# Four graph layers in one kernel: order edges in layer 0, matmuls on zeros ahead of it, and a weight fold spread between transposes

## The chip, the cores and the metric

The kernel runs on one NeuronCore of one Trainium2 chip. The metric is the device time of one execution in microseconds, as a median over runs. "PE" is the matrix engine (TensorE), "DVE" the vector engine, "ACT" the scalar engine, "POOL" GpSimd, and "SP" the engine whose queue issues most of the transfers. "PEclk" is the share of the full clock that the chip granted the PE.

## What is computed

The inputs are x (128 graphs, 64 nodes, 256 features) and adj (128, 64, 64). Four residual layers follow each other, each ending in a layernorm over the features:

- Layer 0: five groups of nodes (one of 25 nodes, the others of 9, 7, 6 and 6), all among the first 25. Each group has its own two-layer graph convolution on the group's part of adj, with weights W1 (256 to 512) and W2 (512 to 256). The outputs are weighted by softmax(fusion_w) and added into the group's nodes.
- Layer 1: one graph convolution with the whole normalised adjacency.
- Layer 2: a polynomial of degree three in the row-normalised adjacency, with a leaky ReLU.
- Layer 3: five rounds of messages, each a GRU cell: gates from `m @ w_ih.T` and `h @ w_hh.T`, where m is the sum over neighbours of `h @ weight[l]`.

The core of layer 0:

```
def _graph_conv(x, adj, W, b):
    A = adj + jnp.eye(n)
    deg = jnp.sum(A, axis=-1)
    dinv = jnp.where(deg == 0, 0.0, deg_safe ** (-0.5))
    norm_adj = dinv[:, :, None] * A * dinv[:, None, :]
    support = jnp.einsum('bnd,de->bne', x, W)
    out = jnp.einsum('bnm,bme->bne', norm_adj, support) + b
    return jax.nn.relu(out)
```

All arithmetic is in f32.

## The kernel before

**Layer 0 in units.** The graphs of a group are cut into units of up to four tiles (class Unit): several graphs' nodes stand below each other on up to 126 partitions. There are 16 units, in the order of the groups 1, 2, 3, 4, 0: three, two, two, two and seven of them. For each unit these steps run:

- `load0`: the group's rows of adj into tile a (three buffers) and of x into xg (six buffers). The loads go out from SP's queue, for units 0 to 2 xg from POOL's; unit 0 uses ACT's queue for half of its a loads.
- `prep`: on DVE, ae = a + identity (L374), its row sums deg, their inverse root (L118 to L124, with a power on POOL, L122), ae scaled (L382), and A0, the block-diagonal matrix of the tile's graphs, made by a multiplication with the constant block0 (L385). The PE transposes A0 (pT, L393), and DVE scales and evicts it to AT (L397). The list `evictions` holds these instructions, `powers` the powers.
- `aggregate`: pa = x times the adjacency (PE, L407), copied by ACT to ag (L412).
- `hidden`: ph = W1 times ag (PE, L422), ReLU by ACT to hg (L425).
- `support`: ps = hg times W2 (PE, L436), copied by ACT to s (L442).
- `add`: po = s times the adjacency (PE, L458), ReLU by ACT to z (L462), added on DVE to F (L469, L480).
- `finish`, for group 0 only: z transposed back (pse, L493), added to x, layernorm, and stored to xa.

The loop is a software pipeline: in iteration i the PE gets add(i-1), aggregate(i+1), support(i), finish(i-1), prep(i+2), hidden(i+1), in this order. Between these it places, from unit 9 on, the steps of layers 1 and 2 for the first two chunks (`early`, that is mid(0) and mid(1); a chunk is eight graphs). Beside the loop stand the layernorms of the nodes 25 to 63 (`others`, tiles xo, one in most iterations), which go out to xb. mid(c) begins with the whole adjacency of its chunk (a64, loaded at L190): Ab (L225), its mask A01 (L231), rsum (L233), then dg (L243) and, on ACT, poly (L247).

**After layer 0.** `fold()` forms V[l], the product of weight[l] and w_ih, in 15 steps (products pf, PE L546; copies by ACT to w, L685, and following). `factors` then forms, for each, sums that the GRU's matrix products use: three on DVE (L662, L664, L665) and one on POOL (L663). The same is done for w_hh. Then come the first states' transposes (`state_of_layer2`, pT L757) and the first messages (pa, L209), chunk by chunk, and the GRU loop, whose first matmul is called parz (L716).

**What sets the order.** The order on the PE is the program's, written by hand. On the other engines a scheduler orders by dependencies and priority; `tc.issue_after(x)` adds an edge that makes an instruction stand after x, and `tc.high_priority()` moves one forward. Each engine then works through its own order and waits at each instruction until that one's inputs have come. PSUM banks come from two pools in rotation (`psum0`).

Of the kernel before, what the change touches and what calls it, by code (L numbers as in the profile page):

```python
# [9 lines left out]
F32 = mybir.dt.float32  # L10
# [51 lines left out]
NU = len(UNITS)  # L62
XP = 40
EPS_LN = 1e-5


@with_exitstack
def gnn_stack(
# [41 lines left out]

        return const(bass.AP(tensor=src.tensor, offset=src.offset, ap=[[0, 128], [1, n]]), [128, n], name, eng, pool)

    powers, evictions = [], []

    def inv_sqrt(v, n, p, name):

# [215 lines left out]
    with ExitStack() as c0:  # L332
# [9 lines left out]
        def load0(i, after=None):  # L342

            u = UNITS[i]

            qa = [nc.scalar, nc.sync] if i == 0 else [nc.sync]
            qx = nc.gpsimd if i < 3 else nc.sync
            a = work.tile([TR, 4, NJ], F32, name="a", bufs=3)
            xg = work.tile([TR, 4, D], F32, name="xg", bufs=6)
            for t, (b0, nb) in enumerate(u.tiles):  # L350
                b = slice(b0, b0 + nb)
                row = 0
                for f, m in RUNS[u.g]:
                    rows = slice(row, row + nb * m)
                    row += nb * m
                    w = u.n if u.g < 2 else NE
                    qa[t % len(qa)].dma_start(a[rows, t, :w], adj[b, f : f + m, 0:w])
                    with tc.issue_after(after.ins) if after else nullcontext():
                        qx.dma_start(xg[rows, t, :], x[b, f : f + m, :])
            loads[i] = a, xg  # L360

        def prep(i):

            u = UNITS[i]
            a, xg = loads.pop(i)
            ae = work.tile([TR, 4, NJ], F32, name="ae", bufs=2)
            A0 = work.tile([TR, 4, TR], F32, name="A0", bufs=1)
            AT = work.tile([TR, 4, TR], F32, name="AT", bufs=4)
            p = psum0("pT").rearrange("p (t n) -> p t n", t=4)
            scale = []  # L370
            for ts, nb, r, k in u.same:
                w, c = ts.stop - ts.start, 0
                for f, m in [(0, u.n)] if u.g < 2 else RUNS[u.g]:
                    nc.vector.tensor_add(  # L374
                        ae[:r, ts, c : c + m], a[:r, ts, f : f + m], eye0[:r, k, None, c : c + m].to_broadcast([r, w, m])
                    )
                    c += m
                av = ae[:r, ts, : u.n]
                deg = small.tile([TR, w], F32, name="deg")
                nc.vector.tensor_reduce(deg[:r], av, AX.X, ALU.add)  # L380
                dinv = inv_sqrt(deg[:r], w, r, "d0")
                nc.vector.tensor_mul(av, av, dinv[:, :, None].to_broadcast([r, w, u.n]))  # L382
                o, c = 0, 0
                for _, m in RUNS[u.g]:
                    nc.vector.tensor_mul(  # L385
                        A0[:r, ts, o : o + nb * m].rearrange("p t (b n) -> p t b n", n=m),
                        ae[:r, ts, None, c : c + m].to_broadcast([r, w, nb, m]),
                        block0[:r, None, k, o : o + nb * m].rearrange("p t (b n) -> p t b n", n=m)
                        .to_broadcast([r, w, nb, m]),
                    )  # L390
                    o, c = o + nb * m, c + m
                for t in range(ts.start, ts.stop):
                    nc.tensor.transpose(p[:r, t, :r], A0[:r, t, :r], ident[:r, :r])  # L393
                scale.append((AT[:r, ts, :r], p[:r, ts, :r], dinv[:, :, None].to_broadcast([r, w, r])))
            for v in scale:
                with tc.high_priority():
                    evictions.append(nc.vector.tensor_mul(*v))  # L397
            A[i] = AT, xg
# [16 lines left out]
        def hidden(i):  # L415
            u = UNITS[i]
            ag0 = AG.pop(i)
            hg = keep.tile([128, 4, 512], F32, tag="NI", name="hg", bufs=2)
            for e in range(4):
                p = psum0("ph")[:, : u.cols]  # L420
                for k in range(2):
                    nc.tensor.matmul(  # L422
                        p, W1[:, u.g, k, e * 128 : (e + 1) * 128], ag0[:, k, : u.cols], start=k == 0, stop=k == 1
                    )
                nc.scalar.activation(hg[:, e, : u.cols], p, AF.Relu, bias=b1[:, u.g * 4 + e : u.g * 4 + e + 1])  # L425
            HG[i] = hg

        def support(i):
# [84 lines left out]

        def others(i):

            layernorm(XO[i], n=XO[i].shape[1])

        def store_others(i):
            t = XO.pop(i)
            nc.sync.dma_start(xb[:, NP * i : NP * i + t.shape[1], :], t)  # L520

        eye0 = const(c_eye0, [TR, 5, NJ], "eye0", nc.scalar, w0)
        load0(0)
        ident = const(c_ident, [128, 128], "ident", nc.scalar)
        block0 = w0.tile([TR, 5, TR], F32, name="block0")
        for ks in (slice(1, 2), slice(2, 5), slice(0, 1)):
            nc.scalar.dma_start(block0[:, ks], c_block0[:, ks])
        nc.vector.memset(F, 0.0)
        b1 = const(b1T, [128, NG * 4], "b1", nc.scalar, w0)
# [35 lines left out]
        for i in range(-2, NU + 1):  # L565
# [21 lines left out]
            if i == -2:  # L587
                load0(1, powers[0])
                load_second(1)
                load0(2, powers[0])  # L590
                load_first(2)
            elif i == -1:
                load_second(2)
                load_first(3)
            elif i == 0:
                load_second(3)
                for g in (4, 0):
                    load_first(g)
                    load_second(g)
            early_stage(i, 2)  # L600
            for f, j in ((store_others, i - 1), (others, i), (load_others, i + 2)):
                for o in range(10):
                    if min(o + 1, 9) == j:
                        f(o)
            if i == -1:

                with tc.issue_after(evictions[0].ins):
                    fm = small.tile([128, 1], F32, name="fm")
                    nc.vector.tensor_reduce(fm, fw, AX.X, ALU.max, negate=True)
                    fe = small.tile([128, NG], F32, name="fe")  # L610
                    nc.scalar.activation(fe, fw, AF.Exp, bias=fm)
                    fs = small.tile([128, 1], F32, name="fs")
                    nc.vector.reduce_sum(fs, fe, axis=AX.X)
                    fr = small.tile([128, 1], F32, name="fr")
                    nc.vector.reciprocal(fr, fs)
                    gw = w0.tile([128, NG], F32, name="gw")
                    nc.vector.tensor_scalar(gw, fe, fr, None, op0=ALU.mult)
                    gb2 = w0.tile([128, NG, 2], F32, name="gb2")
                    nc.vector.tensor_mul(gb2, b2c.rearrange("p (g k) -> p g k", k=2), gw[:, :, None].to_broadcast([128, NG, 2]))
            elif i == 1:  # L620
# [8 lines left out]
                    bhh = const_later(bhhT, [128, 6], "bhh")  # L629
                    mask = const_later(maskT, [128, B // 2], "mask")  # L630
                brz = wp.tile([128, 4], F32, name="brz")
                nc.vector.tensor_add(brz, bih[:, 0:4], bhh[:, 0:4])
            elif i == 4:

                ih = keep.tile([128, 4, 2, D], F32, tag="RZ", name="ih", bufs=2)
                wl = keep.tile([128, 4, 2, D], F32, tag="RZ", name="wl", bufs=2)
# [20 lines left out]
    WHH = work.tile([128, 3, 7, 128], F32, name="WHH")  # L657
    V = [work.tile([128, 3, 7, 128], F32, name=f"V{l}") for l in range(L)]

    def factors(w, w21):  # L660

        nc.vector.tensor_add(w[:, 4, :], w21, w[:, 3, :])  # L662
        nc.gpsimd.tensor_sub(w[:, 6, :], w[:, 0, :], w21)  # L663
        nc.vector.tensor_sub(w[:, 5, :], w[:, 4, :], w[:, 0, :])  # L664
        nc.vector.tensor_sub(w[:, 2, :], w[:, 1, :], w[:, 5, :])  # L665

    raw21 = []

    def fold():
        w21 = work.tile([128, 3, 128], F32, name="wh21")  # L670
        raw21.append(w21[:, 2, :])
        wv = whhT.rearrange("(k p) (q e) -> k p q e", p=128, q=3)
        nc.gpsimd.dma_start(w21, wv[0, :, :, 128:])
        for k in range(2):
            nc.gpsimd.dma_start(WHH[:, :, k, :], wv[k, :, :, :128])
        nc.gpsimd.dma_start(WHH[:, :, 3, :], wv[1, :, :, 128:])
        for l in range(L):
            for q in range(3):
# [2 lines left out]
                nc.scalar.copy(w[:, 0:2, :], p[:, :, 0:128])  # L681
                nc.scalar.copy(w[:, 3, :], p[:, 1, 128:256])
                kept = l == L - 1 and q == 2
                v21 = work.tile([128, 128], F32, name="kept21") if kept else work.tile([128, 128], F32, name="w21", bufs=2)
                nc.scalar.copy(v21, p[:, 0, 128:256])  # L685
                if kept:
                    raw21.append(v21)
# [59 lines left out]
    class Chunk:  # L747
# [12 lines left out]
        def state_of_layer2(self, k):  # L760
            if k:
                self.hT = work.tile([128, 2, NP * 128], F32, tag="hT", name="hT", bufs=4)
            p = self.transpose(lambda q, k: self.xt[:, q, k * 128 : (k + 1) * 128], k, "pT3")
            nc.scalar.copy(self.hT[:, k, :], p)
            if not k:
                self.th = sums(self.hT, "h")

# [122 lines left out]
    rows = []  # L890
    weights = fold()
    for c in (0, 1):
        for _ in range(6):
            next(weights)
        rows.append(Chunk(c))
        rows[c].state_of_layer2(1)
        rows[c].state_of_layer2(0)
        rows[c].messages()
    for _ in weights:
        pass  # L900
# [128 lines left out]
```

## Time and profile before

The median is 2215.38 us (three runs, 2215.13 to 2219.1); the profiled execution spans 2216.7 us.

| stretch, us | what runs | PE busy | DVE busy | ACT busy | PEclk | DMA share |
|---|---|---|---|---|---|---|
| 0 to 60 | layer 0, units 0 to 2 | 46.19 | 25.03 | 17.01 | 1.00 | 0.61 |
| 60 to 140 | layer 0, groups 2 to 4 | 73.23 | 42.87 | 24.03 | 0.94 | 0.58 |
| 140 to 320 | group 0, first steps of layers 1 and 2 | 180.00 | 87.26 | 66.55 | 1.00 | 0.13 |
| 320 to 352 | fold, first states | 29.69 | 25.42 | 13.18 | 0.95 | 0.15 |
| 352 to 2190 | GRU loop | 1838.00 | 1174.63 | 874.19 | 1.00 | 0.03 |
| 2190 to 2217 | end of the last chunk | 14.35 | 18.97 | 8.88 | 0.83 | 0.12 |

How to read it: busy time is the time in which an engine has an instruction running. In the rows of a timeline the first two numbers are the start and the length; then come the engine, the line of the kernel, the operation, the tiles (written from read), their sizes, the number of instructions gathered into the row and, in brackets, the idle time before it and what ended it. In a row of waits the three numbers are the total, the count and the longest.

### The profile page before, as it was taken

The numbers are of one execution on the slowest core, as the hardware profiler recorded it, in microseconds if no ns is written. First come the engines' busy times: TensorE is split into PE (matmuls) and PEld (weight loads), VectorE is DVE, ScalarE is ACT, GpSimd is POOL, SyncE is SP. The second block draws the span as 40 slices with busy tenths as digits, with TensorE's granted clock in tenths as the row PEclk, the third lists the DMA queues.
The fourth block names the chain that finished last, engine by engine and source line by source line (L and its number), as shares of the span: only waits on it lengthen the run. The fifth ranks groups of instructions, "written<-read, shape, count | busy, mean of one in ns | idle before, by whom it ended". The sixth has DMA issues, their size and how long they took to land.

```text
span 2216.7 us, 30151 instructions
## 1 busy us (share of the span) xinstructions
PE 2181.5 (98%) x11530; PEld 1913.5 (86%) x11530; DVE 1374.2 (62%) x3069; ACT 1003.8 (45%) x1853; POOL 578.5 (26%) x639
## 2 busy tenths in 40 slices
PE   7999999999999999999999999999999999999997
PEld 5677888888898889888889898888898898888886
DVE  4443567666666666666766676657666666566546
ACT  2333334445544444445454454455454544455453
POOL 3210123222222223223222222222222232232221
PEclk9999999999999999999999999999999999999999
DMA  6540210000100000000100010001000000000000
GB/s 188 168 129 19 61 46 3 1 3 1 38 4 3 1 20 22 4 1 1 41 1 3 1 41 1 4 1 41 1 1 1 20 10 1 1 10 10 1 1 20
DMA packets 54172, 51.12 MB, mean 23 GB/s; under 512 B 20878, under 2 KB 49036, under 8 KB 54028
## 3 DMA queue, kind: packets, MB, share of 16 engines
q1 hardware_dynamic: 49524, 43.90, 6.5%
q0 software_dynamic: 1936, 4.83, 0.7%
q8 instruction: 91, 1.49, 0.3%
q10 hardware_dynamic: 2568, 0.47, 0.1%
q14 instruction: 53, 0.43, 0.1%
HBM read 32.40 MB, written 16.78 MB: 22 GB/s over the span
## 4 chain that ended last, share of the span: by engine, by line
PE 91%; DMA 3%; DVE 2%; issue 1%; SPq 1%; POOL 1%; ACT 0%; ACTq 0%; POOLq 0%; DVEq 0%
PE parz L716 25%; PE pdrz L716 12%; PE pan L716 12%; PE pa L209 9%; PE pbrz L716 6%; PE pdn L716 6%; PE pT L757 4%; PE pbn L716 3%; PE ps L436 3%; PE pd L306 2%; PE pd L285 2%; PE ph L422 2%; DMA xo<-in_x_dram 1%; PE pa L407 1%; PE po L458 1%
## 5 line engine op out<-in xcount | busy, mean ns | idle before, releaser
L733 ACT COPY c<-parz 128x512 f32<-128x512 f32 x240 | 140.6, 586 | 323.4 <-PE parz L716 322.8
L716 PE MATMUL parz<-Th,WHH 128*128 128x256 f32 x960 | 285.9, 379 | 0.3 <-ACT c L733 0.3
L716 PE MATMUL parz<-Ta,V 128*128 128x256 f32 x960 | 285.5, 379 | 0.0
L696 POOL TENSOR_TENSOR Th<-hn 128x512 f32<-128x512 f32 x64 | 81.4, 1273 | 774.3 <-DVE hn L818 588.6
L815 ACT ACTIVATE NI<-NI,bih 128x512 f32<-128x512 f32 (+1 forms) x162 | 115.9, 715 | 203.7 <-DVE NI L810 203.5
L733 ACT COPY c<-pan 128x512 f32<-128x512 f32 x237 | 138.9, 586 | 149.2 <-PE pan L716 149.2
L716 PEld LDWEIGHTS parz<-Ta,V 128*128 128x128 f32 x960 | 182.4, 190 | 24.8
L716 PEld LDWEIGHTS parz<-Th,WHH 128*128 128x128 f32 x960 | 176.2, 190 | 21.4 <-ACT c L733 0.7
L787 ACT ACTIVATE RZ<-RZ,brz 128x512 f32<-128x512 f32 x160 | 116.0, 726 | 138.9 <-DVE RZ L745 138.9
L696 POOL TENSOR_TENSOR Ta<-agg 128x512 f32<-128x512 f32 x80 | 101.9, 1274 | 260.8 <-ACT agg L213 260.8
L745 DVE TENSOR_TENSOR RZ<-pdrz,c 128x512 f32<-128x512 f32 x80 | 55.1, 688 | 174.1 <-PE pdrz L716 174.1
L716 PE MATMUL pan<-Ta,V 128*128 128x256 f32 x474 | 141.2, 380 | 0.0
L716 PE MATMUL pan<-Th,WHH 128*128 128x256 f32 x474 | 141.0, 379 | 0.0
L138 POOL TENSOR_TENSOR rs<-ve,mhalf 128x4 f32<-128x4 f32 (+3 forms) x67 | 69.0, 1030 | 253.9 <-DVE ve L136 228.2
L739 DVE TENSOR_TENSOR NI<-pbn,c 128x512 f32<-128x512 f32 x79 | 54.7, 692 | 127.7 <-PE pbn L716 108.7
L209 PEld LDWEIGHTS pa<-A,h 128*128 128x128 f32 x1024 | 124.4, 192 | 3.3
L209 PE MATMUL pa<-A,h 128*128 128x128 f32 x1024 | 124.6, 275 | 0.0
L735 DVE TENSOR_TENSOR NI<-pdn,c 128x512 f32<-128x512 f32 x79 | 54.5, 690 | 112.8 <-ACT c L733 112.8
L816 DVE TENSOR_TENSOR RZ<-hn,NI 128x512 f32<-128x512 f32 (+1 forms) x129 | 87.8, 680 | 49.2 <-ACT NI L815 49.2
L818 DVE TENSOR_TENSOR hn<-RZ,NI 128x512 f32<-128x512 f32 (+1 forms) x161 | 109.8, 682 | 1.8
L817 DVE TENSOR_TENSOR RZ<-RZ 128x512 f32<-128x512 f32 (+1 forms) x161 | 109.5, 680 | 1.8
L436 PE MATMUL ps<-W,hg 128*125 128x256 f32 (+5 forms) x464 | 105.6, 385 | 0.0
(217 smaller groups left out, 5077.8 us busy)
## 6 DMA issues: line engine op xcount, KB each, us to landing
out_dram<-xt SPq DMA_DIRECT2D x32, 256.0 KB
W<-in_w_dram SPq DMA_DIRECT2D x10, 512.0 KB
xt<-xb SPq DMA_DIRECT2D x32, 156.0 KB
xo<-in_x_dram SPq DMA_DIRECT2D x9, 512.0 KB
xb<-xo SPq DMA_DIRECT2D x9, 512.0 KB
xt<-xa SPq DMA_DIRECT2D x32, 100.0 KB
xg<-in_x_dram SPq DMA_DIRECT2D x25, 125.0 KB
xa<-xg SPq DMA_DIRECT2D x25, 125.0 KB
```

Of the source, the lines that this page charges most:

```text
L138: nc.gpsimd.tensor_tensor(rs[:r, :n], ve[:r, :n], mhalf[:r, :n], ALU.pow)
L209: nc.tensor.matmul(p[:, q * 128 : (q + 1) * 128], src[:, q, k * 128 : (k + 1) * 128], m[:, q, :], start=True, stop=True)
L436: nc.tensor.matmul(p[: u.rows[t], t - v, :], hg[:, e, u.off[t] : u.off[t] + u.rows[t]], W2[:, u.g, e, :], start=e == 0, stop=e == 3,)
L696: nc.gpsimd.tensor_sub(t[:, 0:2, :], a[:, :, H:], a[:, 0, :].rearrange("p (s n) -> p s n", s=2))
L716: nc.tensor.matmul(bank[:, g, :], w[:, q, i - 1, :], rhs, start=i in (1, 2, 5) and g == 0 and m == 0, stop=m == len(side) - 1, skip_group_ ...
L733: nc.scalar.copy(c, self.a)
L757: nc.tensor.transpose(p[:, q * 128 : (q + 1) * 128], src(q, k), ident)
L787: nc.scalar.activation(RZ[:, q, 0, :], RZ[:, q, 0, :], AF.Sigmoid, bias=b[0])
L815: nc.scalar.activation(n, n, AF.Tanh, bias=bih[:, 4 + j : 5 + j])
L816: e.tensor_sub(d, self.hT[:, j, f], n)
L817: e.tensor_mul(d, d, z)
L818: e.tensor_add(self.hn[:, j, f], d, n)
```

## The change

It leaves the work of layer 0 and of the GRU as it is and alters orders, places and a few engines:

- six matmuls on a tile of zeros go first on the PE, so that it is active while the first loads come;
- the slice of block0 that unit 0 needs goes from ACT's queue to SP's, behind the first two a loads;
- a unit's a loads all go ahead of its xg loads;
- the ae of the next unit, and the layernorm of `others`, get an order edge behind the last AT eviction;
- W1 and W2 of groups 4 and 0 are loaded one per iteration, in 1 to 4, instead of all four in iteration 0;
- the softmax of fusion_w moves from iteration -1 to 0, with its exp behind the first unit's last ReLU;
- the sum brz of two biases moves from iteration 1 to 4;
- the POOL subtraction in `factors` moves to DVE, and the tile w21 gets a third buffer;
- two of six fold steps per chunk are put behind the first states' two sets of transposes, and the copy to hT gets high priority.

```diff
+WARM = 6
@@ load0
+            for rows, t, b, f in runs:
+                qa[t % len(qa)].dma_start(a[rows, t, :w], adj[b, f, 0:w])
+            with tc.issue_after(after.ins) if after else nullcontext():
+                for rows, t, b, f in runs:
+                    qx.dma_start(xg[rows, t, :], x[b, f, :])
@@ prep
-            scale = []
+            scale, last = [], evictions[-1] if evictions else None
...
-                    nc.vector.tensor_add(
-                        ae[:r, ts, c : c + m], a[:r, ts, f : f + m], eye0[:r, k, None, c : c + m].to_broadcast([r, w, m])
-                    )
+                    with tc.issue_after(last.ins) if last else nullcontext():
+                        nc.vector.tensor_add(
+                            ae[:r, ts, c : c + m], a[:r, ts, f : f + m], eye0[:r, k, None, c : c + m].to_broadcast([r, w, m])
+                        )
@@ others
-            layernorm(XO[i], n=XO[i].shape[1])
+            with tc.issue_after(evictions[-1].ins):
+                layernorm(XO[i], n=XO[i].shape[1])
@@ before the loop
+        zero = keep.tile([128, 4, 512], F32, tag="NI", name="zero", bufs=2)[:, 0, :]
+        nc.vector.memset(zero, 0.0)
+        p = psum0("pw")
+        for _ in range(WARM):
+            nc.tensor.matmul(p, zero[:, :128], zero, start=True, stop=True)
         eye0 = const(c_eye0, [TR, 5, NJ], "eye0", nc.scalar, w0)
         load0(0)
+        block0 = w0.tile([TR, 5, TR], F32, name="block0")
+        nc.sync.dma_start(block0[:, 1:2], c_block0[:, 1:2])
         ident = const(c_ident, [128, 128], "ident", nc.scalar)
-        for ks in (slice(1, 2), slice(2, 5), slice(0, 1)):
+        for ks in (slice(2, 5), slice(0, 1)):
@@ in the loop
             elif i == 0:
                 load_second(3)
-                for g in (4, 0):
-                    load_first(g)
-                    load_second(g)
+            elif i < 5:
+                (load_first, load_second)[(i - 1) % 2]((4, 0)[(i - 1) // 2])
...
-            if i == -1:
-
-                with tc.issue_after(evictions[0].ins):
+            if i == 0:
+
+                with tc.issue_after(evictions[1].ins):
...
-                    nc.scalar.activation(fe, fw, AF.Exp, bias=fm)
+                    with tc.issue_after(relus[3].ins):
+                        nc.scalar.activation(fe, fw, AF.Exp, bias=fm)
...
-                nc.vector.tensor_add(brz, bih[:, 0:4], bhh[:, 0:4])
             elif i == 4:
+                with tc.issue_after(evictions[4].ins):
+                    nc.vector.tensor_add(brz, bih[:, 0:4], bhh[:, 0:4])
@@ factors
-        nc.gpsimd.tensor_sub(w[:, 6, :], w[:, 0, :], w21)
+        nc.vector.tensor_sub(w[:, 6, :], w[:, 0, :], w21)
@@ state_of_layer2
-            nc.scalar.copy(self.hT[:, k, :], p)
+            with tc.high_priority():
+                nc.scalar.copy(self.hT[:, k, :], p)
@@ first states
-        for _ in range(6):
+        for _ in range(4):
             next(weights)
         rows.append(Chunk(c))
         rows[c].state_of_layer2(1)
+        next(weights)
         rows[c].state_of_layer2(0)
+        next(weights)
         rows[c].messages()
```

More of the change, by code (lines that the diff above doesn't have):

```diff
@@ L111, in spread @@
         return const(bass.AP(tensor=src.tensor, offset=src.offset, ap=[[0, 128], [1, n]]), [128, n], name, eng, pool)
-    powers, evictions = [], []
+    powers, evictions, relus = [], [], []
     def inv_sqrt(v, n, p, name):
@@ L349, in load0 @@
             xg = work.tile([TR, 4, D], F32, name="xg", bufs=6)
+            w = u.n if u.g < 2 else NE
+            runs = []
             for t, (b0, nb) in enumerate(u.tiles):
-                b = slice(b0, b0 + nb)
                 row = 0
                 for f, m in RUNS[u.g]:
-                    rows = slice(row, row + nb * m)
+                    runs.append((slice(row, row + nb * m), t, slice(b0, b0 + nb), slice(f, f + m)))
                     row += nb * m
[L356 to L359, printed above, removed]
+            for rows, t, b, f in runs:
[3 more added lines that the diff above has]
+                    qx.dma_start(xg[rows, t, :], x[b, f, :])
             loads[i] = a, xg
@@ L424, in hidden @@
                     )
-                nc.scalar.activation(hg[:, e, : u.cols], p, AF.Relu, bias=b1[:, u.g * 4 + e : u.g * 4 + e + 1])
+                relus.append(
+                    nc.scalar.activation(hg[:, e, : u.cols], p, AF.Relu, bias=b1[:, u.g * 4 + e : u.g * 4 + e + 1])
+                )
             HG[i] = hg
@@ L520, in store_others @@
             nc.sync.dma_start(xb[:, NP * i : NP * i + t.shape[1], :], t)
+        zero = keep.tile([128, 4, 512], F32, tag="NI", name="zero", bufs=2)[:, 0, :]
[3 more added lines that the diff above has]
+            nc.tensor.matmul(p, zero[:, :128], zero, start=True, stop=True)
         eye0 = const(c_eye0, [TR, 5, NJ], "eye0", nc.scalar, w0)
         load0(0)
+        block0 = w0.tile([TR, 5, TR], F32, name="block0")
+        nc.sync.dma_start(block0[:, 1:2], c_block0[:, 1:2])
         ident = const(c_ident, [128, 128], "ident", nc.scalar)
-        block0 = w0.tile([TR, 5, TR], F32, name="block0")
-        for ks in (slice(1, 2), slice(2, 5), slice(0, 1)):
+        for ks in (slice(2, 5), slice(0, 1)):
             nc.scalar.dma_start(block0[:, ks], c_block0[:, ks])
@@ L658, in gnn_stack @@
     V = [work.tile([128, 3, 7, 128], F32, name=f"V{l}") for l in range(L)]
+    raw21 = []
     def factors(w, w21):
         nc.vector.tensor_add(w[:, 4, :], w21, w[:, 3, :])
-        nc.gpsimd.tensor_sub(w[:, 6, :], w[:, 0, :], w21)
+        nc.vector.tensor_sub(w[:, 6, :], w[:, 0, :], w21)
         nc.vector.tensor_sub(w[:, 5, :], w[:, 4, :], w[:, 0, :])
         nc.vector.tensor_sub(w[:, 2, :], w[:, 1, :], w[:, 5, :])
-    raw21 = []
     def fold():
         w21 = work.tile([128, 3, 128], F32, name="wh21")
-        raw21.append(w21[:, 2, :])
         wv = whhT.rearrange("(k p) (q e) -> k p q e", p=128, q=3)
         nc.gpsimd.dma_start(w21, wv[0, :, :, 128:])
+        raw21.append(w21[:, 2, :])
         for k in range(2):
@@ L683, in fold @@
                 kept = l == L - 1 and q == 2
-                v21 = work.tile([128, 128], F32, name="kept21") if kept else work.tile([128, 128], F32, name="w21", bufs=2)
+                v21 = work.tile([128, 128], F32, name="kept21") if kept else work.tile([128, 128], F32, name="w21", bufs=3)
                 nc.scalar.copy(v21, p[:, 0, 128:256])
```

## The prediction, made before the changed kernel ran

> **What bounds the kernel now.** I read the page first, then the table of waits of the PE, then the timeline of the PE, then the engines that those waits name. The page and the waits say:
>
> ```profile
> PE 2181.5 (98%) x11530; PEld 1913.5 (86%) x11530; DVE 1374.2 (62%) x3069; ACT 1003.8 (45%) x1853; POOL 578.5 (26%) x639
> ...
> PE pT L393 <- DVE A L385: 9.8, 1, 9.8
> PE pa L407 <- DVE AT L397: 7.5, 4, 4.5
> ...
> PE ph L422 <- ACT ag L412: 3.2, 1, 3.2
> PE pT L757 <- ACT w L685: 2.1, 1, 2.1
> ```
>
> The PE is the bound. All its idle time, but for 4.3 us in the tail and 0.3 in the main loop, lies before the main GRU loop, whose first matmul (parz) starts at 351.83. The order of the PE is fixed by hand, so a microsecond comes off only where the PE idles or runs at half clock. The timeline of the PE gives both (start, length, instructions, idle before):
>
> ```profile
> 9.82 1.10 PE L393 MATMUL pT<-ident,A 126*126 126x126 f32 x4 [9.82 <-DVE A L385]
> 11.70 3.78 PE L407 MATMUL pa<-AT,xg 126*128 126x126 f32 x16 [0.78 <-DVE AT L397]
> 18.69 9.22 PE L422 MATMUL ph<-ag,W 128*128 128x504 f32 x16 [3.21 <-ACT ag L412]
> 27.74 0.59 PE L393 MATMUL pT<-ident,A 126*126 126x126 f32 x4
> ...
> 35.08 1.95 PE L407 MATMUL pa<-AT,xg 126*128 126x126 f32 x16
> ```
>
> The same pT takes 1.10 us at first and 0.59 later, the same pa 3.78 and 1.95; ph takes 9.22 here and 7.03 at 37.18. So the start runs at half clock and pays 0.5 + 1.8 + 2.2 = 4.5 us beside its 13.8 us of idle time. The DVE and ACT timelines name the blockers:
>
> ```profile
> 72.52 0.62 DVE L397 TENSOR_TENSOR AT<-pT,d0o 112x448 f32<-112x448 f32 x1
> ...
> 129.22 0.68 DVE L397 TENSOR_TENSOR AT<-pT,d0o 126x504 f32<-126x504 f32 x1
> ...
> 135.13 0.69 DVE L225 TENSOR_TENSOR Ab<-a,pair 128x512 f32<-128x512 f32 x1 [2.15 <-DMA a<-in_adj_dram]
> ```
>
> ```profile
> 16.57 1.28 ACT L611 ACT_TABLE_LOAD   x1 [16.57 <-DMA fw<-in_fusion_w_dram]
> ```
>
> The AT evictions at 72.52 and 129.22 come 8 to 9 us after their transposes (PE 63.81 and 119.54), behind layernorms of xo that the DVE had been given first. The last fence shows the ACT standing before the fusion softmax until fw lands, although pa, which its next copies wait for, has ended at 15.48.
>
> [...] pairs like 3.78 and 1.95, and records of the granted clock at half for 3.41 us (74.34 to 77.75) and 6.8 us (128.95 to 135.78) after the waits of 1.48 and 4.46. [...] Here SP's issues follow each other every 0.77 us or so from 49 to 130, so a load's place in that queue sets its time.
>
> **The change, part by part.**
>
> Start. The DVE has the first adjacency scaled at 8.20 but waits 0.89 for block, now loaded third on SP; A is then ready at 8.2 + 0.7 = 8.9. The memset of 512 columns costs 3.26 x 512/3840 = 0.43 and lies in the 0.93 that the DVE waits for a at 5.84. The zeros start near 2.2. Six matmuls of ph's size cost 7.03/8 = 0.88 warm, about 1.7 cold. [...] so they end at 9.1 to 10.7; I take 9.9. Then pT 0.44, AT 0.78, pa 1.8, the last ag copy 0.6: ph starts at 13.5 and, with 6.9 warm, ends near 20.4, not 27.74. W1[1] landed at 7.5 and a(1) at 10.7, so they don't bind. Gain 7.4 (6.6 to 8.2). The moved exp costs nothing: ACT's 3 us gap before the first ps covers it.
>
> AT evictions ahead of the xo layernorms. At 73: idle 1.48, pa 2.74 for 1.94, ps 8.07 for 7.07, together 3.3. At 92.86: 0.84 + 0.1 = 0.9. At 129.95: idle 4.46, pa 3.78 for 1.95, ps 6.56 for 5.3, together 7.6. The first two layernorms lose nothing by coming later, as xb is read much later. Gain 11.8.
>
> brz moved. The 12.82 us that the DVE stood for bhh ended at 44.5, and no PE wait came of it. Value 0. The W loads spread over iterations, and the a loads ahead of xg: 0 directly; SP gets through its queue sooner, as its issues were slow from 31 to 43 while four W loads were moving.
>
> Fold. The PE waits 2.13 for an ACT copy of w, held behind DVE and POOL factor sums, and then pays pa 3.10 for 2.05 and pf 11.09 for 10.7; another 0.18 later. Spreading gives 3.7, less about 0.6 for 18 subtractions of 0.28 to 0.48 that now sit on a DVE that is busy for 23.2 of the 28 us from 326 to 354. Gain 3.1.
>
> The main loop: the only reordering is the hT copy between two sigmoids, and the PE is full there. Value 0.
>
> Sum of gains: 7.4 + 11.8 + 3.1 = 22.3.
>
> **The wait added.** The scheduler moves more than the diff says. In the order built for the changed program, layer 1's first steps for chunk 0 stand earlier: on the DVE Ab, rsum and A01, which wait for the a64 adjacency load, now stand between the ae and the A0 of unit 7 (the pT that ran at 119.54), and on the ACT poly, which waits for dg, stands between the two z activations of unit 4, ahead of the ag copies of unit 6. So pT of unit 7 and ph of unit 6 now hang on a64. Before, a64 was issued at 130.1 and landed at 135.0 with nothing pressing behind it. In the new SP order it stands 22 transfers earlier: at 0.77 each, 130.1 - 17 = 113; the smoother start can bring up to 12 more, so 101. Landing is 3 to 4 later: 104 to 117. I take 105.5, nearer the early end, because from 49 on the queue was never held by data. The PE wants that pT at 119.54 - 7.4 - 3.3 - 0.9 = about 107. After landing come Ab 0.69, rsum 0.41, A01 0.42, small ones and A0 0.66: 2.5. Then the column of small ones, An 0.68, dg 0.67 (3 in all), poly 0.72, z 0.72 and two ag copies of 0.38: ph can start 7.6 after landing, at 113.1 where it wants 107.5. That is 5.5 of idle time, and a hole of this size costs about 3 of half clock, as the 4.46 at 129.95 did (1.8 + 1.3). Cost 8.5, from 0 (landing before 100) to 14 + 3 (landing at 114 or later). Queued behind that poly are z, ag, s and hg; the PE waits for all of them.
>
> Net: 22.3 - 8.5 = 13.8, so 2215.4 - 13.8 = 2201.6, about 2201.
>
> **Rivals.**
> - No new wait: a64 lands by 100. For: SP is freed early. Against: even back to back, some 134 transfers of 0.77 take 103 us. Time 2215.4 - 22.3 = 2193.
> - A long new wait: SP goes at its old pace, landing at 114 to 117, cost 14.5 + 3 = 17.5, gain 5: 2207 to 2211, say 2209. For: SP's pace in the profile is steady from 49. Against: it starts its run sooner.
> - Slower: a64 comes as late as before (135)[...]. A0 is then ready at 137.5 where 107 is wanted: 30 + 3 + 3 lost against 22.3, time 2229; halfway, 2219. For: the DVE and ACT are FIFO, so everything stands behind it. Against: nothing in SP's trace waits that long.
> - [...] the start stays half, gain 3 in place of 7.4. Time 2206; inside the range.
>
> **How the numbers follow.** Main case 0.50 (2201); no wait 0.18 (2193); long wait 0.22 (2209), of which a quarter ends within 0.2% (above 2211); slower or held SP 0.10, most of it above 2219.8, the rest in the band. Faster 0.50 + 0.18 + 0.16 = 0.84; same 0.09; slower 0.07. The range runs from below the case without a wait (2191) to just above the long wait (2212).
>
> **What would show it.** pw ending near 10 and pT at once after it; ph of the first unit at full clock, ending near 20; no wait of pa on AT; and near 107 a wait of pT on A, or of ph on ag, with the clock at half after it, the DVE's Ab waiting for DMA, and ACT's poly waiting for dg. The main loop should take 1865 us from parz on as before. The forecast is wrong if a64 lands well off 105, if the zeros delay the first pT, or if the fold's DVE work makes new waits.

## The result, and the profile after

The changed kernel takes 2214.49 us (median of six runs, 2212.88 to 2216.3); the kernel before, on the same chips, 2217.42 (2215.13 to 2219.26). The ratio is 0.9988 with a 95% interval of 0.9975 to 1.0001: a gain of 2.9 us that the measurement can't tell from none. The forecast was 2201, with a range of 2191 to 2212.

The totals of the page hardly move: the PE is busy for 2180.2 us, 2181.5 before. The table of waits of the PE, after the change, does (what waited, for what; total us, times, longest):

```profile
PE pT L397 <- DVE A L389: 15.1, 1, 15.1
PE pT L860 <- DVE hn L834: 4.1, 3, 1.6
PE ph L426 <- ACT ag L416: 2.5, 1, 2.5
PE pf L560 <- ACT w L700: 1.9, 1, 1.9
PE pw L534 <- DVE zero L531: 1.5, 1, 1.5
PE pa L411 <- DVE AT L401: 0.8, 1, 0.8
```

Of the 7.5 us on AT only the first unit's 0.8 is left. The zeros fill most of the 9.8 at the start; the first pT itself comes 1.2 us earlier. In place of these waits stands one of pT on A of 15.1 us, and pf waits where pT waited in the fold. Where the time went is read from the timeline of the PE, by the starts of the same instructions (the first two columns of its rows):

| instruction on the PE | before | after | gained so far |
|---|---|---|---|
| pT of unit 1 | 27.74 | 18.69 | 9.05 |
| pa of unit 5 | 92.86 | 79.60 | 13.26 |
| po of unit 5 | 123.54 | 130.22 | -6.68 |
| ph of unit 7 | 140.48 | 139.64 | 0.84 |
| the last pse but one ahead of the fold | 313.94 | 313.56 | 0.38 |
| parz, the first of the GRU loop | 351.83 | 349.14 | 2.69 |
| end of the span | 2216.7 | 2214.5 | 2.2 |

At 79.60 the kernel is 13.3 us ahead. By 130 it has lost that and 6.7 more; it then regains the 7.5 that the wait at 129.95 had cost before. These are the rows of the PE's timeline around the loss:

```profile
1.49 7.26 PE L534 MATMUL pw<-zero 128*128 128x512 f32 x12 [1.49 <-DVE zero L531]
8.58 0.60 PE L397 MATMUL pT<-ident,A 126*126 126x126 f32 x4
...
11.84 7.02 PE L426 MATMUL ph<-ag,W 128*128 128x504 f32 x16
...
99.18 7.17 PE L442 MATMUL ps<-W,hg 128*126 128x256 f32 x32
121.48 1.10 PE L397 MATMUL pT<-ident,A 126*126 126x126 f32 x4 [15.13 <-DVE A L389]
125.07 5.31 PE L426 MATMUL ph<-ag,W 128*128 128x264 f32 x16 [2.48 <-ACT ag L416]
130.22 1.95 PE L464 MATMUL po<-AT,s 126*128 126x126 f32 x16
```

The first pT now comes at 8.58 at full clock (0.60 us), and ph at 11.84. (Full and half clock are read from the durations here: the trace's record of the granted clock reads 1.00 over the first 60 us of both kernels, also where the old pa took 3.78 us for 1.95.) The pT of unit 7 stands 15.13 us, ph of unit 6 another 2.48, and both then run at half clock (1.10 for 0.60, 5.31 for 3.73; the record of the granted clock reads 0.50 from 111.1 to 127.9, and 1.00 after it). That is 15.13 + 2.48 + 0.5 + 1.6 = 19.7 us. What they wait for is in the timelines of DVE, ACT and SP:

```profile
119.25 0.69 DVE L226 TENSOR_TENSOR Ab<-a,pair 128x512 f32<-128x512 f32 x1 [25.46 <-DMA a<-in_adj_dram]
...
120.68 0.75 DVE L389 TENSOR_TENSOR A<-ae,block 126x252 f32<-126x252 f32 x2
...
122.70 0.68 DVE L244 TENSOR_TENSOR dg<-ident,rsum 128x512 f32<-128x512 f32 x1
```

```profile
123.42 0.72 ACT L248 ACTIVATE poly<-dg,cw 128x512 f32<-128x512 f32 x1 [26.03 <-DVE dg L244]
...
124.65 0.65 ACT L416 COPY ag<-pa 128x264 f32<-128x264 f32 x2
```

```profile
104.39 7.57 SPq L362 DMA_DIRECT2D xg<-in_x_dram  x8
112.00 2.35 SPq L191 DMA_DIRECT2D a<-in_adj_dram  x2
```

The whole chain is here. SP issues a64 at 112.00, behind eight xg loads (of units 10 and 11) that nobody needs yet; the DVE stands 25.46 us at Ab until it lands at 119.25; A of unit 7 follows at 120.68; dg at 122.70; the ACT, which has stood 26.03 us at poly, lets z and the ag copies of unit 6 go; ph starts at 125.07.

### The profile page after: what moved, and what is told of

Same layout as the page of the kernel before. It is cut to its first block, busy times and chain, and to the rows that moved or that the text cites. A ratio compares the mean times of both kernels' runs of the same rounds, so it can differ in the third digit from the quotient of the medians.

```text
span 2214.5 us, 30166 instructions
## 1 busy us (share of the span) xinstructions
PE 2180.2 (98%) x11542; PEld 1911.4 (86%) x11542; DVE 1372.5 (62%) x3088; ACT 1003.1 (45%) x1853; POOL 571.0 (26%) x621
## 3 DMA queue, kind: packets, MB, share of 16 engines
q8 instruction: 91, 1.49, 0.3%
## 4 chain that ended last, share of the span: by engine, by line
PE 94%; SPq 2%; DVE 1%; issue 1%; DMA 1%; ACT 0%; POOL 0%; POOLq 0%; DVEq 0%; ACTq 0%
PE parz L731 25%; PE pdrz L731 12%; PE pan L731 12%; PE pa L210 9%; PE pbrz L731 6%; PE pdn L731 6%; PE pT L772 4%; PE ps L442 4%; PE ph L426 3%; PE pbn L731 3%; PE pd L286 2%; PE pd L307 2%; SPq L362 1%; PE pa L411 1%; PE po L464 1%
```

## The experiments

The theory: the loss is layer 1's first steps on the DVE and ACT, standing in their queues ahead of layer 0's work and waiting for a64. The rivals: SP's pace is the limit and returns any gain; or the gains themselves were not there. The comparisons with the kernel before are each with its runs on the same chips.

| kernel | median us | ratio to before (95%) |
|---|---|---|
| the change | 2214.49 | 0.9988 (0.9975 to 1.0001) |
| e1_edge | 2201.21 | 0.992 (0.9906 to 0.9935) |
| e2_early | 2212.49 | 0.9974 (0.9963 to 0.9984) |
| e3_edge_nowarm | 2202.88 | 0.9931 (0.9916 to 0.9946) |
| e4_nowarm | 2219.45 | 1.0006 (0.9997 to 1.0015) |
| f1_edge8 | 2199.24 | 0.9911 (0.9894 to 0.9927) |
| f2_oldfold | 2199.14 | 0.9912 (0.9897 to 0.9927) |
| f4_noorder | 2213.79 | 0.9978 (0.997 to 0.9986) |
| f7_fwpool | 2197.93 | 0.9906 (0.9892 to 0.9921) |
| g1_edges_only | 2217.38 | 0.9995 (0.9988 to 1.0002) |
| g2_edges_late | 2206.85 | 0.9946 (0.9931 to 0.996) |
| g3_whh | 2197.56 | 0.9901 (0.9887 to 0.9916) |
| g4_pool | 2201.76 | 0.9918 (0.9901 to 0.9934) |
| g5_rsum_late | 2193.51 | 0.9894 (0.9877 to 0.991) |
| g6_edges_again | 2219.82 (one run) | none |

### The place of Ab taken away (e1, f1)

```diff
 # mid(c), on top of the change; e1: evictions[-1], f1: evictions[11], the last of unit 8
+        with tc.issue_after(evictions[-1].ins) if c < 2 else nullcontext():
             nc.vector.tensor_mul(Ab..., a64..., pair...)
...
+        with tc.issue_after(evictions[-1].ins) if c < 2 else nullcontext():
             nc.vector.tensor_reduce(rsum, a64, AX.X, ALU.add)
```

> One order edge is added to the changed kernel: layer 1's first Ab and rsum (chunks 0 and 1) stand behind the AT eviction of unit 11, so the DVE no longer meets them ahead of the A0 of unit 7. SP's order is untouched, and the a64 load goes out as late as before. Theory (the DVE and ACT stand behind a late a64): the 15.1 us wait of pT on A, the 2.5 of ph on ag and the half clock after them (0.5 + 1.6) go, 19.7 us in all, so 2214.5 - 19.7 = 2195 (2193 to 2198). Rival (the time that was gained in the first 100 us is lost again at the next data that come late, since SP's queue sets the pace): 2208 to 2215.

Measured 2201.21, 13.3 us less than the change. Neither the theory's range nor the rival's holds it, but the table of waits and the PE's starts do side with the theory: no wait of pT on A is left, and pT of unit 7, which stood until 121.48 in the change, runs through:

```profile
108.24 0.60 PE L399 MATMUL pT<-ident,A 126*126 126x126 f32 x4
```

The ph of unit 7 starts at 121.65, where the change has it at 139.64. That is 18.0, or 20.0 when the 2.05 us are taken out by which this execution was already behind at the pT of unit 1 (20.74). SP still issued a64 at 109.34. The rest was lost elsewhere: pa waited 2.2 us for the ACT's v at 250, and at half clock after it ps took 8.50 for 7.07 and pT 0.95 for 0.60. This v had stood 4.50 us for the DVE, which was at those of layer 1's first steps that the edge had now pushed so far back.

> The changed kernel with the order edge of the first Ab and rsum behind the AT eviction of unit 8, not of unit 11: late enough for a64, early enough that poly and the rest of layer 1's first steps don't meet the ACT at 250. Theory: the wait of pa on the ACT copy v (2.2 us) and the transposes' slowness after it (0.5), which the edge behind unit 11 showed, go: 2201.2 - 2.7 = 2198.5 (2196 to 2201, since the start moves by some 2 us between executions). Rival (that wait came from something else): 2201.

Measured 2199.24, as expected; the wait at 250 has gone (pT of layer 1's first step starts at 249.08, not 251.79), and the start was slow here too (pT of unit 1 at 20.55).

### The same place, with a64 there in time (e2)

```diff
+            if i == 2:                       # two loads, some 80 places earlier in SP's queue
+                for c in (0, 1):
+                    load_adj(c)
...
-            elif i == g0:
-                for c in (0, 1):
-                    load_adj(c)
 # and in mid(c): Ab and rsum behind evictions[8], the last of unit 6, where they stood in the change
```

> The changed kernel with Ab and rsum kept exactly where they stand (between the ae and A0 of unit 7, by an order edge behind the AT eviction of unit 6; poly likewise between the two z of unit 4), but with the two a64 loads of chunks 0 and 1 some 80 transfers earlier in SP's queue. Theory (the lateness of the data is the cost, not the place of the instructions): no wait of pT at 106, 2195 (2193 to 2198). Rival (the place itself costs, by the DVE and ACT work that now lies ahead of A0 and ag): 2200 or more.

Measured 2212.49: the sum is the rival's, the trace is not. These are three rows of its DVE:

```profile
91.85 0.67 DVE L227 TENSOR_TENSOR Ab<-a,pair 128x512 f32<-128x512 f32 x1
...
97.45 0.72 DVE L391 TENSOR_TENSOR A<-ae,block 126x252 f32<-126x252 f32 x2
...
121.35 0.42 DVE L236 TENSOR_REDUCE rsum<-a 128x4 f32<-128x256 f32 x1 [18.58 <-DMA a<-in_adj_dram]
```

Ab no longer waits, A of unit 7 is ready at 98.2, and pT of unit 7 runs at 107.07 without a wait: the place alone costs nothing when the data are there. But the next such instruction, rsum of chunk 2, stands a little further on, and its a64 had been left at 118.04 in SP's queue. The DVE stood there for 18.58 us and pa of unit 7 waited 11.92 for its AT. The wait moved one load along.

### The zeros left out (e3, e4)

The six matmuls on zeros go (`WARM = 0`): in e3 on top of e1, in e4 on top of the change.

> The kernel with the added edge, without the six matmuls on zeros. Theory: the first pT, pa and ph run at half clock again, 0.5 + 1.8 + 2.2 = 4.5 us, so about 2199.5 (2198 to 2202) if the edge alone gives 2195. Rival (the PE would have opened the clock within the first pa anyway): 2195 to 2197.

> The changed kernel without the six matmuls on zeros and without the added edge. Theory: the PE stands at pT of unit 7 until a64 has come, and a64 comes by SP's own pace, so the 4.5 us lost at the start only shorten that wait: 2214 to 2217, within 2 us of the changed kernel. Rival (each stage adds its own time): 2219.

e3: 2202.88, 1.7 us above e1, between theory and rival. In e3 pT, pa and ph run at half clock again (pT of unit 1 at 21.85), for about 3 us; but in e1 ph waits 1.36 for ag, since the ACT's copies (the first at 13.25) stand behind the issue of the fusion_w load at 11.56, which takes part of that back. Another part is that the zeros themselves can hold pT up. So most of what the start gained isn't theirs: without them pT of unit 1 starts at 21.85, 5.9 us ahead of the kernel before. Two executions of kernels whose starts are alike, f1 and f2:

```profile
1.49 8.35 PE L536 MATMUL pw<-zero 128*128 128x512 f32 x12 [1.49 <-DVE zero L533]
9.68 0.60 PE L399 MATMUL pT<-ident,A 126*126 126x126 f32 x4
```

```profile
1.50 6.89 PE L536 MATMUL pw<-zero 128*128 128x512 f32 x12 [1.50 <-DVE zero L533]
8.77 0.65 PE L399 MATMUL pT<-ident,A 126*126 126x126 f32 x4 [0.38 <-DVE A L391]
```

The same twelve records last 6.89 to 8.35 us. The first of them start some 0.9 us apart and the last about half of that (in the change two steps from 1.49 to 3.36, and four from 6.44 to 8.2), so the step from half to full clock comes sooner or later among them, to judge by these times; what sets it was not shown. In f1 pT comes only after their end, in f2 it waits for A.

e4: 2219.45, 5.0 us above the change, where I had expected at most 2. One half of the theory held: SP issued a64 at 110.62, and it was in at 117.71, no later than in the change, although the start was slower. The other half failed, for the kernel without the six instructions was built into another order. Its DVE:

```profile
117.71 0.69 DVE L226 TENSOR_TENSOR Ab<-a,pair 128x512 f32<-128x512 f32 x1 [23.75 <-DMA a<-in_adj_dram]
...
119.81 1.38 DVE L154 TENSOR_SCALAR xo<-xo,mv,rs 128x256 f32<-128x256 f32 x4 [0.92 <-POOL rs L139]
...
123.31 0.72 DVE L389 TENSOR_TENSOR A<-ae,block 126x252 f32<-126x252 f32 x2
```

Here a layernorm and its wait for POOL stand between Ab and A too: 5.6 us from one to the other, 1.4 in the change. So e4 doesn't price the zeros.

### The order edges (f4, g1, g2, g6)

f4 takes the edges on ae and on the xo layernorm out of f1; g1 puts these two alone into the kernel before; g2 is g1 with the late edge of f1. g6 is g1 again, for its trace: g1's traced execution took 4683 us, twice as long as any of the other nineteen (2214.61 to 2221.31), and isn't used.

```diff
 # g1, on top of the kernel before
+            scale, last = [], evictions[-1] if evictions else None
...
+                    with tc.issue_after(last.ins) if last else nullcontext():
                         nc.vector.tensor_add(ae..., a..., eye0...)
...
+            with tc.issue_after(evictions[-1].ins):
                 layernorm(XO[i], n=XO[i].shape[1])
```

> The kernel with the edge behind unit 8, with the order edges on ae and on the xo layernorms taken out: AT may stand behind layernorms again. The prediction's step says the three waits of pa on AT come back (3.3 + 0.9 + 7.6 = 11.8): 2210 (2207 to 2212). Rival (the waits of the kernel before came from late xo and W loads, which are now spread, and not from the order): 2199 to 2203.

Measured 2213.79, 14.6 above f1 and 1.8 above the range expected: here the edges are worth at least the 11.8 of the prediction. The waits of pa on AT in its trace are 2.2, 2.6 and 7.7, at 29.90, 70.76 and 129.66. They are back although the W loads are spread, so the rival is out.

> The kernel before with the two order edges alone (ae of the next unit, and the xo layernorm, behind the last AT eviction); nothing else of the change. In its built order Ab and rsum stand ahead of the A0 of unit 7, and poly between the two z of unit 4, as in the changed kernel. Theory (the edges that take the AT waits away are also what put the new wait there): the waits of pT on A and ph on ag near 110 to 125 stand in place of those on AT, with no gain in sum: 2217 to 2223. Rival (the new wait comes from another part of the change): the edges bring their 11.8 us, 2207.

> The kernel before with the two order edges alone, for its trace. Theory: a wait of pT on A of 10 to 15 us and one of ph on ag of 2 to 3 stand between 108 and 130, with Ab on the DVE waiting for a64, and none of pa on AT at 73 or 130: the edges alone put the new wait there, and it cancels them. Rival: no such wait; the AT waits are still there.

g1: 2217.38, ratio 0.9995 (0.9988 to 1.0002): nothing gained. g6's trace shows why, on its DVE and PE:

```profile
118.33 0.69 DVE L225 TENSOR_TENSOR Ab<-a,pair 128x512 f32<-128x512 f32 x1 [16.05 <-DMA a<-in_adj_dram]
```

```profile
120.56 1.10 PE L394 MATMUL pT<-ident,A 126*126 126x126 f32 x4 [5.73 <-DVE A L386]
124.16 6.20 PE L423 MATMUL ph<-ag,W 128*128 128x264 f32 x16 [2.49 <-ACT ag L413]
```

The wait on a64 is there with the two edges alone. It is 5.73 and not 10 to 15, because this PE, with the old start, comes to pT later; the data come at about the same time (118.33 against 119.25). In the built orders, without a run, taking either edge out of the change moves Ab one unit later, behind the A of unit 7, and taking out both moves it behind the A of unit 8, where it stood before.

> The kernel before with the two order edges and, besides, the edge of Ab and rsum behind the AT eviction of unit 8. Theory: the waits of pa on AT are gone and nothing takes their place: 2218.7 less 11.8 (the prediction's sum) to 14.6 (what their removal from the other kernel cost): 2204 to 2207. Rival (the edges help only beside the spread W loads): 2210 or more.

Measured 2206.85, 12.2 under the kernel before: the edges bring what was predicted once Ab stands late. No wait of pa on AT is left in its trace but the first unit's 0.8. The late edge alone on the kernel before wasn't tried; Ab started there at 135.13, after the last of the waits that went.

### The fold (f2, g4, g3)

f2 has the fold of the kernel before on top of f1. g4 and g3 start from f7 (below): g4 has only the subtraction back on POOL, g3 leaves it on DVE and forms the w_hh sums later.

```diff
 # g3
-                if l == 0:
+                if l == 2:
                     factors(WHH[:, q], w21[:, q, :])
```

> The kernel with the edge behind unit 8 and the fold as it was before the change: the subtraction on POOL, two buffers of w21, six products ahead of each chunk's transposes, no priority for the hT copy. The prediction's step says 3.1 us slower than with the changed fold, the trace of the changed kernel (parz against the pse ahead of the fold, 1.8 us nearer than before) says 1.8: 2200 to 2202, and the waits of pT on w (2.1) are back, with the clock at half. Rival (the fold's reorder bought nothing, as DVE and POOL hold each other up): 2198 to 2199.

> The kernel with the edge behind unit 8 and fusion_w on POOL's queue, with the subtraction of the factor sums back on POOL; the spread products, the third buffer of w21 and the hT priority stay. Theory (the move to DVE is the useful part of the fold's change, since POOL has the sums Th and Ta in the same stretch): the copies to w wait longer, 2199 to 2202. Rival (the move only carried the wait over to DVE): 2196 to 2198.5.

> The kernel with the edge behind unit 8 and fusion_w on POOL's queue, with the factor sums of w_hh six fold steps later. In the traces a 128x128 subtraction on DVE takes 0.28 us alone and 0.8 to 2.1 while POOL forms the first sums Th and Ta, and the w_hh sums stand in that stretch ahead of those of V that ACT's copies to w wait for. Theory: the 1.9 us wait of pf on w goes, with up to 1.7 of half clock after it: 2194.5 to 2196.5. Rival (the copies wait for other sums in the same stretch): 2198.

The medians of f2 and f1 are the same (2199.14 and 2199.24). The length from the last pse but one to parz tells more than the whole time:

| fold | us |
|---|---|
| as before: the kernel before; f2; g2; g6 | 37.9; 37.5; 37.7; 40.0 |
| changed: the change, e1 and e4; e2, e3, f1, f4 and f7 | 35.6; 37.2 to 37.4 |
| changed, subtraction on POOL: g4 | 38.7 |
| changed, w_hh sums later: g3 and g5 | 33.4 |

The eight executions of the changed fold have the same wait of pf on w, 1.86 to 2.02. In five of them half clock follows it (in f1 pf 2.70 and 2.50 for 1.99 and 1.89, pT 1.06 for 0.60), in the other three not (in the change the same pf take 1.99 and 1.89, the pT 0.60). So the fold's change was worth some 2 us in these three and 0.1 to 0.7 in the five, against the first three folds of the first row; what decides between the two was not shown. What the wait stands for is to be seen in the change's own DVE and POOL:

```profile
325.26 0.28 DVE L681 TENSOR_TENSOR V<-V 128x128 f32<-128x128 f32 x1
...
327.69 1.36 DVE L681 TENSOR_TENSOR V<-V 128x128 f32<-128x128 f32 x1
...
329.96 2.11 DVE L680 TENSOR_TENSOR WHH<-WHH,wh 128x128 f32<-128x128 f32 x2
...
332.19 0.81 DVE L681 TENSOR_TENSOR V<-V 128x128 f32<-128x128 f32 x1
```

```profile
327.52 1.37 POOL L711 TENSOR_TENSOR Th<-hT 128x512 f32<-128x512 f32 x1
...
330.60 1.32 POOL L711 TENSOR_TENSOR Ta<-agg 128x512 f32<-128x512 f32 x1
```

A 128x128 sum of L681 takes 0.28 us, and 1.36 beside POOL's 1.37, 0.81 beside its shorter ones (0.73 to 0.86); the 2.11 are two sums. The durations show that the two go together, not by what means. The ACT's copies to w wait for these sums (2.67 and 2.98 us at 332.35 and 336.04), and pf for a copy. g3, in which the w_hh sums no longer stand in that stretch, has no wait of pf at all and a fold 3.8 us shorter than f7. So the place of the w_hh sums makes the wait; whether it would be there without their lengthening beside POOL wasn't tried. The median of 2197.56 (2193.98 to 2199.88) missed the expectation nevertheless: in the trace pa of unit 9 waited 3.5 us for AT. The trace of g4 speaks for the move to DVE (with the subtraction on POOL pf waits 3.3), but it also has 3.6 on that AT, so its median isn't the price of the move.

### Where fusion_w is loaded, and the last AT (f7, g5)

```diff
 # f7, on top of f1
-        fw = spread(fusion_w, NG, "fw", w0, nc.scalar)
+        fw = spread(fusion_w, NG, "fw", w0, nc.gpsimd)
 # g5, on top of f7 with g3's edit: rsum of chunks 2 and 3 behind the last AT eviction
+        with tc.issue_after(evictions[11 if c < 2 else -1].ins) if c < 4 else nullcontext():
             nc.vector.tensor_reduce(rsum, a64, AX.X, ALU.add)
```

> The kernel with the edge behind unit 8, with the load of fusion_w on POOL's queue instead of ACT's. In the traces ACT's table load and first ag copies stand behind the issue of that load, [...] (9.15 us in the changed kernel, 11.56 in the one with the edge behind unit 11). Theory: ph of the first unit starts at about 11.8 each time, up to 2 us earlier than otherwise: 2196.5 to 2198.5. Rival (the issue is covered by the PE's own chain): as with the edge alone.

Measured 2197.93 (2196.92 to 2199.18), within the expectation. The wait of ph on ag is gone, but ph starts at 12.66 and not at 11.8, as the zeros lasted 8.07 us here; and as f1's runs span 2198.08 to 2200.22, the 1.3 us between the medians isn't settled.

> The kernel with the edge behind unit 8, fusion_w on POOL's queue and the w_hh sums later, and with rsum of chunks 2 and 3 behind the last AT eviction of layer 0. In the traces of the two kernels without this last edge the DVE stands 7.7 and 10.7 us at chunk 2's rsum for its a64, and the AT of unit 9 behind it is late by 0.6 and 3.5 us. Theory (the same fault, one load further on): the wait of pa on AT near 144 goes, 3.5 and about 1 of half clock: 2197.6 - 4.5 = 2193 (2191 to 2195.5). Rival (AT of unit 9 waits for something else): 2196 to 2199.

Measured 2193.51 (2193.4 to 2194.54), with this table of waits:

```profile
PE pT L862 <- DVE hn L836: 4.3, 3, 1.8
PE pw L536 <- DVE zero L533: 1.5, 1, 1.5
PE pa L413 <- DVE AT L403: 0.8, 1, 0.8
PE parz L733 <- ACT c L750: 0.3, 1, 0.3
PE ps L444 <- ACT v L315: 0.3, 1, 0.3
```

The wait near 144 was chunk 2's rsum, the same fault once more. Ahead of the loop the PE waits 2.6 us in all: for the tile of zeros, for the first AT and once for v. g5 beats both kernels: 0.9894 (0.9877 to 0.991) of the kernel before.

## Why the prediction was wrong

**The start, 7.4: right in size, less so in its parts.** In this execution it brought 9.05 us (27.74 to 18.69). In the ten executions with the zeros (four of them with fusion_w on POOL's queue) pT of unit 1 starts between 18.69 and 20.74, so 7.0 to 9.05 us earlier than in the trace of the kernel before. The zeros ended at 8.75 here and by 9.84 at the latest, where the prediction says "I take 9.9", an estimate of mine that the trace of before does not show. Their own share is smaller than the 4.5 us of half clock of the old start: 1.7 between e3 and e1. The rest is block0, the ACT and the order of the loads, which were not tried one by one. ("a(1) at 10.7" is misread: its first reader starts at 11.94, having waited 0.29 for it. It bound nothing.)

**The AT waits, 11.8: right.** In the change 3.2 at 73, 1.0 at 93 and 7.5 at 130; 12.2 in g2 and 14.6 in f4.

**brz, W loads:** put at nothing on the PE, and no wait of the PE came or went by their name. They were not tried alone, so this isn't shown.

**The fold, 3.1: over-sized.** In this execution it is 2.3 in its own stretch (37.9 to 35.6), and 1.8 from unit 7's ph to parz (0.84 to 2.69), as 0.5 were lost ahead of it; between f1 and f2 about 0. The step put the 18 subtractions on the DVE at some 0.6, without a working. The wait of 1.87 took the old one's place: the w_hh sums stood ahead of those that the copies need, and sums took up to 1.36 beside POOL.

**The main loop, 0: right**: from parz to the end 1864.9 before, 1865.4 after. (The PE is idle for some 12 us in the last row of the table of stretches; the 4.3 of the prediction are its waits there, and the rest comes after its last matmul.)

**The wait added, 8.5: this step failed.** The mechanism was as written: Ab and rsum ahead of unit 7's A, poly ahead of z and ag. The size was 19.7. The PE came to pT at 106.4, as forecast (107), and from landing to ph there were 5.8 us (7.6 forecast). The term that was mis-sized is the landing, "I take 105.5": it was 119.25. Two parts of it were wrong.

- The issue. The "smoother start", which "can bring up to 12 more", brought next to nothing: in the twelve traces with a64 at this place in SP's queue its issue lies at 107.9 to 114.2, with quick and slow starts at either end, and 113 at the old pace was the right reading of the timeline. A landing at 105.5 asks for an issue near 102, but the prediction's own line against the first rival excludes that: 134 transfers of 0.77 take 103 us. In the five of these traces in which SP never pauses by as much as 0.5 us ahead of a64, its issue lies at 107.9 to 110.9, which is 0.80 to 0.82 for each of the 134. In the change SP also stood 3.65 us at 87.02, which the trace puts down to a load of wl.
- The landing. "Landing is 3 to 4 later" should have been 7.2 (112.00 to 119.25; 7.1 in e4 and g6). The kernel before had shown 4.9 (130.1 to 135.0, as the prediction itself says), and I used less.

With 113 and 4.9 the same working gives a landing at 118 and a cost of 18 + 3 = 21, so 2214. That this is the measured time is in part luck: 7.6 and 3 were too much (5.8 and 2.1), the landing still too early, and the 2215.4 of three runs is 2 us under the median of six (2217.42).

The rival "a long new wait" described what came and had 0.22, but its sum doesn't follow from its landing: by the same working 117 costs 17 + 3 = 20, not 14.5 + 3, and gives 2213, above the end of the range.

The sum of the gains, 22.3, is met by this trace: 9.05 + 4.2 + 7.5 + 1.85 = 22.6, where a start that came out well makes up for the fold. By the medians it was too high: f1, the change with the new wait taken away, is 19.5 under the kernel before. g5 comes to 2193.5, where the rival "no new wait" had 2193, but with two edits that the change doesn't have (fusion_w on POOL's queue, the w_hh sums later), so that this agreement is luck too.

Why the landing takes 7.2 us here and 4.9 before was not tried.

## What to carry to other kernels

Look at every instruction that an order edge lets move up, not only at those that it was meant for: a load's first reader, moved ahead of urgent work in an engine's order, makes that load urgent (here the DVE stood 25.46 us at one, and the ACT behind it 26.03, with urgent work next in their orders). Two edges that each removed a real wait brought nothing until one more edge held the next layer's first reader back, and then 12 us. And take a load's time from its place in its queue and from a landing that the trace shows; where the queue issued back to back, 0.80 to 0.82 us for each of 134 transfers, a faster start elsewhere didn't bring it forward.

## What was not expected of the hardware

- With the same wait of 1.9 us the same fold took 35.6 us in three executions and 37.2 to 37.4 in five: half clock follows the wait in the five and not in the three. Without the wait it took 33.4 (g3, g5).
- A DVE sum of two 128x128 tiles goes from 0.28 to 1.36 us beside one POOL subtraction of 1.37 us, so that work moved from a busy POOL to the DVE was still drawn out while POOL worked.
- The issue of a64 hardly moved with the start of the kernel: 107.9 to 114.2 us over twelve traces, with the first matmuls on data at full or at half clock. In the five of them without a pause in SP's queue the limit was the queue itself, at 0.80 to 0.82 us for each of 134 transfers.
